# All four LSTM gates as a tanh, three in one activation, with doubled states, and another order of two loads

## The chip, the cores and the metric

The kernel runs on one core of one Trainium2 chip. The metric is the device time of one execution in microseconds (us), given as the median of several runs. Engines: PE (TensorE: matmuls, PEld are its weight loads), DVE (VectorE), ACT (ScalarE), POOL (GpSimd) and SP (SyncE). SP, ACT and POOL also issue DMAs.

## The reference

The input x has 1250 rows of 512, and there is a list of 20,000 edges (src, dst). Each row is normalised, goes through a two-layer graph network (sums over edges, two 512x512 weight products per layer), and is added to x. The result, normalised again, is the input sequence of an LSTM with 1250 steps, batch 1 and 512 hidden values; its outputs are added and returned. The LSTM is what the change touches:

```python
combined = jnp.concatenate((x_t, h_prev), axis=1)
f_t = jax.nn.sigmoid(combined @ W_f + b_f)
i_t = jax.nn.sigmoid(combined @ W_i + b_i)
c_tilde = jnp.tanh(combined @ W_c + b_c)
c_t = f_t * c_prev + i_t * c_tilde
o_t = jax.nn.sigmoid(combined @ W_o + b_o)
h_t = o_t * jnp.tanh(c_t)
```

## The kernel before, in words

**Graph part (0 to about 390 us).** Edge counts are built as matmuls of one-hot rows, then two layers of aggregation (L784) and weight products (L176). During it POOL and SP load the input weights Wx of the four gates and their biases bx (`load_wx`, L570 and L572); POOL's next own instruction after these is the first write to xp_d.

**The LSTM in 32 stretches.** The 1250 rows are cut into 32 stretches of 40 that run side by side, as a batch of 32. Each stretch begins 96 steps ahead of its own rows so that its state settles: 12 steps without the recurrent product (BEFORE) and 84 with it (WARM). So there are 84 + 40 = 124 full steps, n = -84 to 39. At the end the kept states of neighbouring stretches are compared against TOL; `far` holds the count of values further apart, and only if that count is over 0 does the branch of L1094 run all 1250 steps in order (`in_order`). Every engine reads that count (L1092) for the branch.

**Input products.** The product of the normalised rows with Wx is made in 40 units: 10 tiles of 128 rows, each with 4 quarters of the 512 hidden values. `multiply(u)` makes one on PE (8 matmuls at L970, and four transposes per tile at L888). `put(u, part)` adds the bias on DVE (L980) and splits the result into three bf16 planes: L982 on ACT, L986 on DVE, L987 on ACT, L989 on DVE, one waiting for the other; then POOL writes them to xp_d in DRAM (L990). `fetch(n)` on SP (L855) reads the planes of one step n back for all stretches. It must wait until all four quarters of a tile are written. At most five fetched steps are held.

**The stretch before the recurrence.** The order of all engines in the LSTM is written out by hand. The first 19 units (AHEAD) run alone; from unit 7 on, each has one of the 12 steps without recurrence beside it: PE opens it from a fetched step (L1003), ACT applies tanh and sigmoid (L1010, L1012), DVE updates the cell (L1014, L1015), and then the splitting of the unit before follows on the same engines. At the end of each iteration ACT issues one of 16 loads of the recurrent weights Wh (L618, 256 KB each; gate by gate, four parts a gate). The first full step reads all of Wh.

**A full step.** The 512 hidden values lie as four column groups of 32 partitions with 128 values each, cut into two halves s = 0, 1 of 64. `open_gates` (L630) brings in the input products, `add_gates` (L638) adds the recurrent product in eight blocks. The blocks come in the order

```python
for b, s in ((0, 0), (1, 0), (0, 1), (2, 0), (3, 0), (1, 1), (2, 1), (3, 1)):
```

where blocks b = 0, 1 read hT[0], the transposed output of the first half, and b = 2, 3 read hT[1]. So the three blocks up to (0, 1) need hT[0] alone, the next wants hT[1], the gates of the first half are complete after five blocks, and those of the second after eight. Each block is 4 matmuls in two passes, 8 matmul records. Then `cell` runs for each half: ACT tanh of gate c (L645), sigmoid of f and i (L647), sigmoid of o (L649); DVE two products in one instruction (L651), their sum (L652); ACT tanh of the new state (L654); DVE the output (L655) and its transpose to hT (L656). DVE and ACT work strictly in this order, so the second half's L651 stands behind the first half's L656. For the first 21 full steps (units 19 to 39) a `multiply` and a `put` stand beside the step. From n = 0 on DVE also adds the output to the rows (L1089), and rows are stored in six groups (L865), the last after the last step.

**Places.** `gates` (L149) sets the order of the gates in Wx, bx, Wh and in the step's PSUM tile: f, i, o, c. The state cg holds two blocks of 64: cell state and tanh of c.

Of the kernel before, what the change touches and what calls it, by code (L numbers as in the profile page):

```python
# [38 lines left out]
def gnn_lstm_kernel(  # L39
# [44 lines left out]
    def rsqrt(pool, v, out, name):  # L84
# [9 lines left out]
        nc.vector.tensor_scalar(q, q, -0.5, 1.5, OP.mult, OP.add)  # L94
# [54 lines left out]
    gates = [(W_f, b_f), (W_i, b_i), (W_o, b_o), (W_c, b_c)]  # L149
# [6 lines left out]
    def layernorm_scale(pool, mv, out, name):  # L156
        ve = pool.tile([R, mv.shape[1]], F32, name=name + "_v")
        nc.vector.tensor_scalar(ve, mv[:, :, 1], EPS, None, OP.add)
        rsqrt(pool, ve, out, name)
# [47 lines left out]
    with ExitStack() as gnn_stack:  # L207
# [358 lines left out]
        def load_wx(pool):  # L566
            Wx = pool.tile([128, KD, NG, D], F32, name="Wx")
            bx = pool.tile([R, NG, D], F32, name="bx")
            for g, (W, b) in enumerate(gates):
                (nc.sync if g % 2 else nc.gpsimd).dma_start(  # L570
                    Wx[:, :, g, :], W[:D, :].rearrange("(k p) n -> p k n", p=128))
                nc.gpsimd.dma_start(bx[:, g, :], row_bcast(b, R))  # L572
            return Wx, bx
# [21 lines left out]
        def rstd_of(pool, t0, n):  # L595
            layernorm_scale(pool, mv2[:, t0:t0 + n, :], rstd2[:, t0:t0 + n], f"lx{t0}")
# [14 lines left out]
        def load_wh(pool):  # L611
# [11 lines left out]
            return Wh, [lambda g=g, j=j: part(g, j) for g in range(NG) for j in range(4)]  # L623
# [17 lines left out]

        def cell(pool, p, cg, s, hh, hT):

            m = slice(64 * s, 64 * (s + 1))
            nc.scalar.activation(cg[:, 1, :], p[:, 3, :], AF.Tanh)  # L645
            sg = pool.tile([128, 2, 64], F32, name=f"sg{s}")
            nc.scalar.activation(sg, p[:, 0:2, :], AF.Sigmoid)  # L647
            so = pool.tile([128, 64], F32, name=f"so{s}")
            nc.scalar.activation(so, p[:, 2, :], AF.Sigmoid)  # L649
            pr = pool.tile([128, 2, 64], F32, name=f"pr{s}")  # L650
            nc.vector.tensor_mul(pr, sg, cg)  # L651
            nc.vector.tensor_add(cg[:, 0, :], pr[:, 0, :], pr[:, 1, :])  # L652
            th = pool.tile([128, 64], F32, name=f"th{s}")
            nc.scalar.activation(th, cg[:, 0, :], AF.Tanh)  # L654
            nc.vector.tensor_mul(hh[:, m], so, th)  # L655
            nc.vector.transpose(hT.rearrange("p b c -> p (b c)"), hh[:, m])  # L656

        def in_order(pool, ps_g, Wh):

            cgs = [pool.tile([128, 2, 64], F32, name=f"cgs{s}") for s in range(2)]  # L660
# [4 lines left out]
            with tc.For_i(0, N, 1) as t:  # L665
# [20 lines left out]
                nc.vector.tensor_add(xr, xr, hh)  # L686
# [6 lines left out]
        def general():  # L693
# [64 lines left out]
            with tc.tile_pool(name="any_lstm", bufs=1) as anyp, \  # L758
                    tc.tile_pool(name="any_ps", bufs=1, space=PSUM) as ps_g:
                Wh, parts = load_wh(anyp)  # L760
                for part in parts:
                    part()
# [130 lines left out]
        def lstm(first_yT, Wx, bx, Wh, wh_parts, close_wx):  # L893
# [7 lines left out]
            TOL, CHECK = 2.0 ** -18, 3  # L901
# [7 lines left out]
            with ExitStack() as pools:  # L909
# [7 lines left out]
                cgs = [seq.tile([128, 2, 64], F32, name=f"cg{s}") for s in range(2)]  # L917
# [79 lines left out]
                cx = some.tile([128, 2, 128], F32, name="cx")  # L997
# [9 lines left out]
                def step_before(final):  # L1007

                    p = opened.pop(0)
                    nc.scalar.activation(cx[:, 1, :], p[:, 3, :], AF.Tanh)  # L1010
                    sg = some.tile([128, 2, 128], F32, name="sgx")
                    nc.scalar.activation(sg, p[:, 0:2, :], AF.Sigmoid)  # L1012
                    pr = some.tile([128, 2, 128], F32, name="prx")
                    nc.vector.tensor_mul(pr, sg, cx)  # L1014
                    nc.vector.tensor_add(cx[:, 0, :], pr[:, 0, :], pr[:, 1, :])  # L1015
# [3 lines left out]
                    nc.scalar.activation(pr[:, 0, :], p[:, 2, :], AF.Sigmoid)  # L1019
                    nc.scalar.activation(pr[:, 1, :], cx[:, 0, :], AF.Tanh)  # L1020
                    nc.vector.tensor_mul(hh, pr[:, 0, :], pr[:, 1, :])
# [5 lines left out]
                with tc.manual_schedule(engines={mybir.EngineType.PE, mybir.EngineType.DVE,  # L1027
                                                 mybir.EngineType.Activation, mybir.EngineType.Pool,
                                                 mybir.EngineType.SP}):

                    nc.scalar.activation(warm, ones, AF.Sigmoid)
# [13 lines left out]
                    for u in range(AHEAD):  # L1045
# [10 lines left out]
                        for part in wh_parts[u:u + 1]:  # L1056
# [4 lines left out]
                    for n in range(-WARM, LEN):  # L1061
# [25 lines left out]
                        if n >= 0:  # L1087

                            nc.vector.tensor_add(x2c[:, n, :], x2c[:, n, :], hh)  # L1089
                            if n + 1 in stores:  # L1090
                                store(x2c, ([0] + stores)[stores.index(n + 1)], n + 1)
                n_far = nc.values_load(far, min_val=0, max_val=128 * 8 * 31)  # L1092
# [14 lines left out]
        def fast():  # L1107
            with ExitStack() as side, ExitStack() as right:
# [13 lines left out]
                Wh, parts = load_wh(late)  # L1122
                lstm(first_yT[0], Wx, bx, Wh, parts, right.close)
# [35 lines left out]
```

## Time and profile before

| | us |
|---|---|
| median of 3 runs | 1097.77 (1097.53 to 1098.74) |
| the profiled execution, whole | 1097.48 |
| its span, first to last instruction | 1095.7 |
| PE busy | 1008.4 (92%) |
| DVE busy | 520.5 (48%) |
| ACT busy | 342.8 (31%) |
| POOL busy | 57.9 (5%) |
| PE busy from 471.0 to 629.6 | 156.7 of 158.6 |
| PE busy from 629.6 to 1085.5 | 399.3 of 455.9 |
| granted TensorE clock, mean | 0.992 |

How to read the rows that follow. A row of a group gives line, engine, operation, written tile <- read tiles, partitions x elements, count, then busy time in us, mean ns of one, and after the second bar the idle time of that engine just before these instructions, with what ended it. A row in order of time gives start in us, length in us, and in square brackets how long the engine had been idle and who released it; PEld rows show when PE's weight loads begin, which is when the data for the matmuls was there. Matmul ends are modelled, so a busy PE may hold small gaps. A wait row gives the total, the number and the longest. "adj", "planes", "S" and "h" are names of memory that the LSTM uses again for its own tiles.

### The profile page before, as it was taken

Reading aid. Unit: us, or ns where it says so; the run is one execution under the profiler, and the core shown is the slowest. Engines: PE = TensorE matmul, PEld = TensorE weight load, DVE = VectorE, ACT = ScalarE, POOL = GpSimd, SP = SyncE. Lnnn points to the kernel's source line nnn. Section 1 sums busy time; section 2 is a strip of 40 time slices with the busy share of each in tenths; the row PEclk is TensorE's granted clock in tenths of the full one; section 3 lists DMA queues with packets and bytes.
Section 4 is the critical chain, followed back from the end, with each engine's and each line's share of the span. In section 5 each row is a group of like instructions: output and inputs, shape, how many; then the busy total and the mean of one; then the engine's idle time right before and its main releaser. Section 6 shows DMA issues by size and latency. Waiting matters only on the chain.

```text
span 1095.7 us, 26606 instructions
## 1 busy us (share of the span) xinstructions
PE 1008.4 (92%) x10972; PEld 520.2 (47%) x10988; DVE 520.5 (48%) x1800; ACT 342.8 (31%) x1268; POOL 57.9 (5%) x96
## 2 busy tenths in 40 slices
PE   7999999999999998999999988888888888888886
PEld 4555554554455443344444444444444444444443
DVE  7887676003300765655554544444444444444444
ACT  3321224204301024433333333333333333333332
POOL 0000001000000011111101070000000000000000
PEclk9999999999999999999999999999999999999999
DMA  8100001500200047663323383333333333434441
GB/s 251 50 1 1 0 1 69 204 1 25 69 1 1 0 126 245 188 186 101 95 90 109 102 227 103 89 91 90 91 96 89 88 88 89 109 82 123 108 96 21
DMA packets 38227, 98.51 MB, mean 90 GB/s; under 512 B 5796, under 2 KB 11756, under 8 KB 38094
## 3 DMA queue, kind: packets, MB, share of 16 engines
q1 hardware_dynamic: 28208, 68.67, 22.7%
q0 software_dynamic: 7168, 23.60, 6.3%
q10 hardware_dynamic: 2718, 4.42, 1.3%
q8 instruction: 89, 1.46, 0.5%
q14 instruction: 44, 0.36, 0.1%
HBM read 74.29 MB, written 19.76 MB: 86 GB/s over the span
## 4 chain that ended last, share of the span: by engine, by line
PE 50%; issue 26%; DVE 13%; ACT 7%; DMA 1%; SPq 1%; POOL 1%; DVEq 0%; ACTq 0%; POOLq 0%
PE gates L638 29%; PE psM L970 8%; PE psM L176 8%; DVE adj L651 3%; ACT adj L654 3%; DVE hT L656 3%; DVE adj L655 2%; DVE cg L652 2%; ACT cg L645 2%; PE acc L441 2%; ACT adj L647 2%; DVE od L427 1%; POOL xp_d L990 1%; PE gates L630 1%; DVE ob L425 1%
## 5 line engine op out<-in xcount | busy, mean ns | idle before, releaser
L638 PE MATMUL gates<-Wh,hT 128*32 128x256 f32 x7936 | 457.6, 381 | 58.3 <-DVE hT L656 58.1
L638 PEld LDWEIGHTS gates<-Wh,hT 128*32 128x32 f32 x7936 | 233.4, 109 | 254.1 <-DVE hT L656 119.6
L651 DVE TENSOR_TENSOR adj<-adj,cg 128x128 f32<-128x128 f32 x248 | 68.2, 275 | 222.9 <-ACT adj L647 222.5
L970 PE MATMUL psM<-Wx,xT 128*128 128x512 f32 x320 | 147.4, 606 | 0.6 <-DVE adj L980 0.6
L784 PE MATMUL agg<-adj,planes 128*128 128x512 bf16 (+1 forms) x704 | 129.1, 343 | 2.7 <-DVE x L489 1.9
L645 ACT ACTIVATE cg<-gates 128x64 f32<-128x64 f32 x248 | 55.4, 223 | 213.5 <-PE gates L638 209.9
L654 ACT ACTIVATE adj<-cg 128x64 f32<-128x64 f32 x248 | 63.6, 256 | 129.5 <-DVE cg L652 129.5
L784 PEld LDWEIGHTS <-planes 128*128 128x128 bf16 x720 | 70.4, 98 | 62.4 <-DVE x L489 2.7
L655 DVE TENSOR_TENSOR adj<-adj 128x64 f32<-128x64 f32 x248 | 55.9, 225 | 79.9 <-ACT adj L654 79.9
L970 PEld LDWEIGHTS psM<-Wx,xT 128*128 128x128 f32 x320 | 58.7, 192 | 71.3 <-issue 69.0
L656 DVE STREAM_TRANSPOSE hT<-adj 128x64 f32<-128x64 f32 x248 | 60.8, 245 | 23.7 <-DVE adj L655 0.9
L647 ACT ACTIVATE adj<-gates 128x128 f32<-128x128 f32 x248 | 67.2, 271 | 0.1
L652 DVE TENSOR_TENSOR cg<-adj 128x64 f32<-128x64 f32 x248 | 55.8, 225 | 8.5
L176 PE MATMUL psM<-w,hT 128*128 128x512 f32 x128 | 58.6, 610 | 0.0
L649 ACT ACTIVATE adj<-gates 128x64 f32<-128x64 f32 x248 | 57.0, 230 | 0.0
L427 DVE TENSOR_SCALAR od<-ids,key 125x820 f16<-125x820 f16 (+42 forms) x160 | 55.5, 347 | 0.0
L630 PE MATMUL gates<-h,sel 96*32 96x256 bf16 x992 | 50.3, 273 | 0.1
L990 POOL DMA_DIRECT2D xp_d<-planes x40 | 28.7, 718 | 408.2 <-issue 214.3
L441 PE MATMUL acc<-od,ob 125*128 125x400 f16 (+22 forms) x360 | 46.1, 260 | 3.6 <-DVE od L427 3.2
L425 DVE TENSOR_SCALAR ob<-ids,low 125x128 f16<-125x128 f16 x160 | 39.5, 247 | 13.5 <-PE acc L441 13.2
L982 ACT CAST planes<-adj 128x512 bf16<-128x512 f32 x40 | 24.7, 618 | 60.7 <-DVE adj L980 60.7
L630 PEld LDWEIGHTS <-sel 96*32 96x32 bf16 x992 | 26.6, 97 | 35.2 <-issue 16.4
(165 smaller groups left out, 704.6 us busy)
## 6 DMA issues: line engine op xcount, KB each, us to landing
h<-xp_d SPq DMA_DIRECT2D x136, 384.0 KB, 4.1
xp_d<-planes POOLq DMA_DIRECT2D x40, 384.0 KB, 3.3
base<-x POOLq DMA_DIRECT2D x40, 64.0 KB, 4.6
w<-in_L_gnn_w_dram SPq DMA_DIRECT2D x2, 1024.0 KB
w<-in_L_gnn_w_dram POOLq DMA_DIRECT2D x2, 1024.0 KB, 5.9
xp_d<-planes SPq DMA_DIRECT2D x10, 144.0 KB, 2.9
h<-in_x_dram SPq DMA_DIRECT2D x10, 128.0 KB, 2.6
h<-in_x_dram SPq DMA_DIRECT2D x10, 120.0 KB, 2.8
```

Of the source, the lines that this page charges most:

```text
L176: nc.tensor.matmul(p, lT[:, k, :], rhs[:, k, :], start=(k == 0), stop=(k == KD - 1))
L630: nc.tensor.matmul(ps[s][32 * j:32 * (j + 1), :, :], lhs(j), rhs(j, s), start=True, stop=False)
L638: nc.tensor.matmul(ps[s][32 * j:32 * (j + 1), :, :], hT[b // 2][:, b % 2, :], Wh[:, b, :, 128 * j + 64 * s:128 * j + 64 * (s + 1)], start= ...
L645: nc.scalar.activation(cg[:, 1, :], p[:, 3, :], AF.Tanh)
L647: nc.scalar.activation(sg, p[:, 0:2, :], AF.Sigmoid)
L651: nc.vector.tensor_mul(pr, sg, cg)
L652: nc.vector.tensor_add(cg[:, 0, :], pr[:, 0, :], pr[:, 1, :])
L654: nc.scalar.activation(th, cg[:, 0, :], AF.Tanh)
L655: nc.vector.tensor_mul(hh[:, m], so, th)
L656: nc.vector.transpose(hT.rearrange("p b c -> p (b c)"), hh[:, m])
L784: nc.tensor.matmul(p[:, :n * R], planes[:, k, pl, f * 128:(f + 1) * 128], adj[:, k, t0:t0 + n, :].rearrange("b i r -> b (i r)"), start=(k ...
L970: nc.tensor.matmul(p, yT[n][:, k, :], quarter(Wx[:, k, :, :], j), start=(k == 0), stop=(k == KD - 1))
```

## The change

Four things are done.

1. **Gates as a tanh.** sigmoid(z) = (1 + tanh(z/2)) / 2. All gates are now tanh with a constant scale, the cell state is kept as 2c and the output as 2h. To make one scale serve all gates, the pre-activations come out as 2z for f, i, o and 4z for c: rstd2 is doubled, bx is doubled, and for gate c Wx, bx and Wh are doubled once more. The order of gates becomes f, i, c, o, so that f, i, c are next to each other: one activation writes all three into cg, which has four blocks now (state, f, i, c). Gate o has an activation of its own, as before. DVE's products, sum, output and the adding to the rows become scalar_tensor_tensor (two operations with a constant in one instruction); their number is the same. The tolerance of the comparison doubles with the states.
2. **Doublings.** POOL doubles bx and the parts for gate c right after their loads (three instructions). ACT doubles Wh's part for gate c in four instructions, one at the end of each of units 4 to 7. In the built order the fourth stands between unit 7's splitting and the next step without recurrence.
3. **Loads of Wh.** Two parts at the end of each of units 0 to 4 (gate c first), none in units 5 to 10, one in each of units 11 to 16. Before: one in each of units 0 to 15.
4. **The count.** Every engine reads `far` after the last step's adding and before the last stores; before, after them.

In the built program one activation table for tanh is loaded in the stretch before the recurrence, in place of two (tanh, then sigmoid). W_c moves from SP's to POOL's queue and W_o the other way, since the gates alternate.

```diff
-    gates = [(W_f, b_f), (W_i, b_i), (W_o, b_o), (W_c, b_c)]
+    gates = [(W_f, b_f), (W_i, b_i), (W_c, b_c), (W_o, b_o)]
+    C, O = 2, 3
...
+            for v in (bx, bx[:, C, :], Wx[:, :, C, :]):
+                nc.gpsimd.tensor_scalar(v, v, 2.0, None, OP.mult)
...
+            def double(b):
+                nc.scalar.activation(Wh[:, b, C, :], Wh[:, b, C, :], AF.Copy, scale=2.0)
...
+        def inner(p, cg, pr, so=None):
+            nc.scalar.activation(cg[:, 1:4, :], p[:, 0:3, :], AF.Tanh, scale=0.25)
+            if so is not None:
+                nc.scalar.activation(so, p[:, O, :], AF.Tanh, scale=0.25)
+            nc.vector.scalar_tensor_tensor(pr, cg[:, 1:3, :], 1.0, cg[:, 0:4:3, :],
+                                           op0=OP.add, op1=OP.mult)
+            nc.vector.scalar_tensor_tensor(cg[:, 0, :], pr[:, 0, :], 0.5, pr[:, 1, :],
+                                           op0=OP.mult, op1=OP.add)
+        def outer(hh, cg, so, th):
+            nc.scalar.activation(th, cg[:, 0, :], AF.Tanh, scale=0.5)
+            nc.vector.scalar_tensor_tensor(hh, so, 1.0, th, op0=OP.add, op1=OP.mult)
+        def add_rows(x, hh):
+            nc.vector.scalar_tensor_tensor(x, hh, 0.5, x, op0=OP.mult, op1=OP.add)
...
         def cell(pool, p, cg, s, hh, hT):
-            nc.scalar.activation(cg[:, 1, :], p[:, 3, :], AF.Tanh)
-            sg = pool.tile([128, 2, 64], F32, name=f"sg{s}")
-            nc.scalar.activation(sg, p[:, 0:2, :], AF.Sigmoid)
             so = pool.tile([128, 64], F32, name=f"so{s}")
-            nc.scalar.activation(so, p[:, 2, :], AF.Sigmoid)
             pr = pool.tile([128, 2, 64], F32, name=f"pr{s}")
-            nc.vector.tensor_mul(pr, sg, cg)
-            nc.vector.tensor_add(cg[:, 0, :], pr[:, 0, :], pr[:, 1, :])
             th = pool.tile([128, 64], F32, name=f"th{s}")
-            nc.scalar.activation(th, cg[:, 0, :], AF.Tanh)
-            nc.vector.tensor_mul(hh[:, m], so, th)
+            inner(p, cg, pr, so)
+            outer(hh[:, m], cg, so, th)
             nc.vector.transpose(hT.rearrange("p b c -> p (b c)"), hh[:, m])
...
-            TOL, CHECK = 2.0 ** -18, 3
+            TOL, CHECK = 2.0 ** -17, 3
...
                 def step_before(final):
                     p = opened.pop(0)
-                    nc.scalar.activation(cx[:, 1, :], p[:, 3, :], AF.Tanh)
-                    sg = some.tile([128, 2, 128], F32, name="sgx")
-                    nc.scalar.activation(sg, p[:, 0:2, :], AF.Sigmoid)
                     pr = some.tile([128, 2, 128], F32, name="prx")
-                    nc.vector.tensor_mul(pr, sg, cx)
-                    nc.vector.tensor_add(cx[:, 0, :], pr[:, 0, :], pr[:, 1, :])
+                    inner(p, cx, pr)
...
-                        for part in wh_parts[u:u + 1]:
+                        for part in wh_parts[2 * u:2 * u + 2] if u < 5 else wh_parts[u - 1:u]:
+                            if u < 5 or u > 10:
+                                part()
+                        for part in wh_doubles[u - 4:u - 3] if u >= 4 else ():
                             part()
...
                         if n >= 0:
-                            nc.vector.tensor_add(x2c[:, n, :], x2c[:, n, :], hh)
+                            add_rows(x2c[:, n, :], hh)
+                            if n + 1 == LEN:
+                                n_far = nc.values_load(far, min_val=0, max_val=128 * 8 * 31)
                             if n + 1 in stores:
                                 store(x2c, ([0] + stores)[stores.index(n + 1)], n + 1)
-                n_far = nc.values_load(far, min_val=0, max_val=128 * 8 * 31)
```

In the new kernel the wide activation stands at L654, the output gate's at L656, the products at L657, the sum at L659, the tanh of the state at L664, the output at L665 and the transpose at L678.

## The prediction

> **What bounds the kernel now.** I read the page for the lines that carry time, then PE's waits by stretch, then one step in order of time. The last half of the span is the recurrence: 124 steps. 21 of them (471 to 630 us) have 3.6 us of input products beside them; PE then lacks 1.9 us in all, so nothing off PE counts there. The other 103 (n = -63 to 39) do not:
>
> ```profile
> L638 PE MATMUL gates<-Wh,hT 128*32 128x256 f32 x7936 | 457.6, 381 | 58.3 <-DVE hT L656 58.1
> ...
> L645 ACT ACTIVATE cg<-gates 128x64 f32<-128x64 f32 x248 | 55.4, 223 | 213.5 <-PE gates L638 209.9 <-PE gates L630 0.6
> ...
> L647 ACT ACTIVATE adj<-gates 128x128 f32<-128x128 f32 x248 | 67.2, 271 | 0.1
> ```
>
> PE waits 58 us for the transposes L656, ACT 210 us for PE: a loop, each waiting for the other. One step in order of time (start, length):
>
> ```profile
> 807.29 1.88 PEld L638 LDWEIGHTS gates<-Wh,hT 128*32 128x32 f32 x40 [0.31 <-DVE hT L656]
> ...
> 808.49 0.22 ACT L645 ACTIVATE cg<-gates 128x64 f32<-128x64 f32 x1 [1.86 <-PE gates L638]
> 808.61 0.27 ACT L647 ACTIVATE adj<-gates 128x128 f32<-128x128 f32 x1
> ...
> 808.91 0.29 DVE L651 TENSOR_TENSOR adj<-adj,cg 128x128 f32<-128x128 f32 x1 [1.68 <-ACT adj L647]
> ...
> 809.24 0.22 DVE L652 TENSOR_TENSOR cg<-adj 128x64 f32<-128x64 f32 x1
> ...
> 809.79 0.23 DVE L655 TENSOR_TENSOR adj<-adj 128x64 f32<-128x64 f32 x1 [0.32 <-ACT adj L654]
> ...
> 810.12 0.25 DVE L656 STREAM_TRANSPOSE hT<-adj 128x64 f32<-128x64 f32 x1
> ...
> 810.29 0.25 DVE L651 TENSOR_TENSOR adj<-adj,cg 128x128 f32<-128x128 f32 x1
> ```
>
> The reader is to see two loops. **First half:** hT[1] reaches PE at 807.29, ACT starts at 808.49, hT[0] reaches PE at 810.42 (3.12 after 807.29); PE then needs 6 groups of 4 matmuls (0.24 + 5 x 0.216 = 1.32) before it wants hT[1]: 4.44 round. **Second half:** 807.29, ACT at 809.78 (ten groups), L651 at 810.29, hT[1] at 811.74: 4.45 round, the step's period. L651 of the second half starts right behind the transpose of the first (810.12 + 0.17), 0.08 later than its activations would allow. So a gain in the first half moves both.
>
> **The steps: three activations become two.** ACT start to L651 is 0.42: L647 starts 0.12 behind L645, takes 0.27, and 0.03 passes. After, one activation of 192 per row stands there. The trace has no such width. The same PSUM form just behind a wait takes 224 ns at 64 (L645), 278 at 128 (L1010), 384 at 256 (L1012): 0.83 ns an element, so 192 takes 331 ns, an estimate from these rows, and L651 starts 0.36 behind: **0.061 us less**. The output gate's own activation still ends (0.46) long before L665 reads it. Bounds: the 64-to-128 step as L645 and L647 show it (224, 271) gives 318 and 0.074 less; an activation that reads SBUF (L1020, 301 at 128) would take 354 at 192, and 0.038 less. I take 331, on the line of three rows of the same form.
>
> The DVE instructions stay four. Three become scalar_tensor_tensor with constants:
>
> ```profile
> L928 DVE TENSOR_TENSOR S<-S 128x248 f32<-128x248 f32 x1 | 0.4, 418 | 0.0
> L929 DVE SCALAR_TENSOR_TENSOR S<-S 128x248 f32<-128x248 f32 x1 | 0.4, 418 | 0.0
> ...
> L187 DVE SCALAR_TENSOR_TENSOR w<-ident,w 128x128 f32<-128x128 f32 x16 | 3.5, 285 | 10.6 <-ACT w L181 10.6
> ```
>
> Same time at 248 a row, and 285 at 128 against 291 for L651: cost nothing. The strided operand (tanh and state, three blocks apart) is read in rows of 64 as before. Each new instruction waits for the same engines as the one it replaces. The scale constants are part of the activation: L482 (scale a constant, 2048 a row) at 1906 ns fits 0.83 ns an element and 0.2 fixed. add_rows is a DVE instruction like L1089 (250 ns), with over 1 us of idle DVE behind it.
>
> Both loops shorten by 0.061: the first half by its activation, the second because the transpose it stands behind comes earlier (its activations would allow 2.86 after 807.29; the transpose allows 2.93). Next late is the same loop; PE's own work per step is 3.73 of 4.39. 103 x 0.061 = **6.3 us** (3.9 by 0.038, 7.6 by 0.074).
>
> [...]
>
> **The stretch before the recurrence (391 to 471 us).** PE makes products, DVE and ACT split them, POOL writes them to xp_d, SP fetches them.
>
> ```profile
> PE pc L1003 <- DMA h<-xp_d: 4.6, 3, 2.8
> PE psM L970 <- DVE adj L980: 0.6, 1, 0.6
> ```
>
> First what PE waited for (total, times, longest), then rows in order of time:
>
> ```profile
> 412.33 1.28 ACT L1010 ACT_TABLE_LOAD   x1
> ...
> 413.92 1.28 ACT L1012 ACT_TABLE_LOAD   x1
> ...
> 432.00 0.57 PE L1003 MATMUL pc<-h,sel 96*32 96x512 bf16 x4 [2.80 <-DMA h<-xp_d]
> 432.50 5.18 PE L970 MATMUL psM<-Wx,xT 128*128 128x512 f32 x8
> ```
>
> Tanh and sigmoid each load a table at 412; with tanh alone one goes (1.28) and the two activations of a step become one (384 a row, about 0.48 against 0.28 + 0.38 + gaps). L1014 comes at 414.1, not 415.63; the 0.6 wait of PE goes. What is late next: L980, L982, L986, L987 and L989 of the same unit follow, then the fourth doubling of Wh, which stands on ACT ahead of the next activation. A doubling is one 128x512 activation, 0.62 (L248). The other three fall into gaps of 1.4 us in front of L982; this one takes 0.6 of the 1.5 gained. The last write of tile 1 to xp_d then leaves about 1.05 earlier than 424.04, and the fetch behind it, which PE waits for at 432.00, lands about 1.05 earlier. After that the same chain runs on: PE's waits of 2.80 and 1.32 stay nearly as long. **1.1 us.**
>
> The uneven Wh loads I cost at nothing: packets of a fetch come 1.3 to 1.4 us after its issue whether a Wh load went just before (407.9, 427.1, 446.2) or not (463.9). Two loads per unit up to unit 4 can delay the write that the first fetch waits for, by at most the 256 KB added, 0.9 us at the 300 GB/s that this stretch reaches; that is the lower bound (0.2 left). Above: behind the wait of 2.80 the products run at half pace (a unit of 5.18, else 3.6), behind that of 1.32 they don't. The wait shrinks to 2.5; if that is short enough, 1.5 us more. I take the nearer row, 2.80.
>
> [...]
>
> POOL's doubling of Wx and bx (4608 a row; by masks' select at 285 ns for 128, 10 us) starts when the last bx load has landed (209 us). Behind it on POOL is L990 at 394.7, and PE's first use is at 386.6: 165 us of cover. W_c and W_o trade the SP and POOL queues, both landed by 209.
>
> **The end.** SP issues its last store until 1091.95, then reads the count (TENSOR_LOAD 0.60, checks, branch at 1092.98), then walks 20 semaphores to the end. Read early, SP does it while it waits for the last row, and ACT behind its last activation (1089.08, done by 1090.0, and its first store goes at 1090.14 anyway). SP comes 0.96 earlier to its semaphores; but the last store, issued at 1091.77, lands 1.8 later, 1093.58, between the second and third of them, so part is waited for again. Between 0 and 0.96; I take **0.4**.
>
> Sum: 6.3 + 1.1 + 0.4 = 7.8. The profiled execution took 1097.48 (span 1095.7 and 1.78 around it): 1089.7. It lies 0.29 under the median of 1097.77: **1090.0 us**.
>
> **Rivals.**
> - *The clock stays up.* The wait for the second fetch, 2.5 in place of 2.80, no longer halves the pace of the products behind it: 1.5 us more, 1088.5. For it: 1.32 didn't; against: 2.80 is nearer. 0.20. [...]
> - *The uneven loads free the fetches.* With no Wh load from unit 5 to 10 they land in time, and PE's waits (4.6 + 0.6) and the half pace (1.5) go: 6.7 in place of 1.1, 1084.4. For it: the 16 DMA engines are full from 410 to 418 and 430 to 438 us; against: the fetch issued at 463.9, with no Wh load near, took as long. 0.10.
> - *The step does not follow.* Another wait takes the place: the second half's L651 stays where it is, so only the stretch before and the end gain, 1.5: 1096.3. For it: that L651 waits behind a transpose, not behind ACT; against: that transpose moves too. 0.05.
> - *Slower: the three DVE instructions cost more than those they replace.* Each lies on both loops. L265 and L586 (a column as scalar) take 747 to 750 at 512 a row, L986 692: 0.055 more. With that, 3 x 0.055 - 0.061 = 0.104 a step: 10.7 us slower, less 1.5: 1107.0. It decides from 0.025 each. Against: L929 and L187 show nothing. 0.03.
> - *It does not do what it says.* The rounding of the tanh form leaves states apart by more than the tolerance, and all 1250 steps run in order, at no less than 4.4 us: over 6,600 us in all. 0.02.
>
> The forecast itself 0.60. Its bounds are 3.9 + 0.2 + 0 = 4.1 (1093.7) and 7.6 + 2.6 + 1.0 = 11.2 (1086.6), the first rival's within them; all ends at once are unlikely above, and the second rival lies below: 1085.5 to 1093.5. What a measurement can tell from no change is 0.2%, 2.2 us. Faster 0.92, same 0.03 (from the third rival), slower 0.05.
>
> **What would show it.** Right: plain steps 4.39 apart; the wide activation 331 ns and L657 0.36 behind its start; L657, L659, L665 at 291, 225, 225; one table load at 412; the second fetch wait about 2.5; no TENSOR_LOAD on SP behind the last store. Wrong: a step over 4.43, L657 longer than 0.30, more than 5 us of fetch waits, or PE matmuls of the first step waiting for Wh.

## The result, and the profile after

| | before | after |
|---|---|---|
| median, us | 1097.91 (1097.53 to 1098.74, 4 runs) | 1089.07 (1087.37 to 1090.95, 4 runs) |
| the profiled execution, whole | 1097.48 | 1087.95 |
| its span | 1095.7 | 1086.0 |
| granted clock, mean | 0.992 | 0.994 |

The ratio is 0.9921 (95% interval 0.9909 to 0.9934): 8.8 us faster. The forecast was 1090.0, with a range of 1085.5 to 1093.5. Five more runs of the changed kernel on another chip gave a median of 1090.5 (1090.34 to 1091.18), again 0.9922 (0.9908 to 0.9936).

The two spans differ by 9.7 us. Cut at the same events of both traces (first Wh load, transposes of the first half of a step):

| stretch | before | after | gain | forecast |
|---|---|---|---|---|
| start to the first Wh load | 390.83 | 390.33 | 0.50 | 0 |
| to the first full step's transpose | 85.20 | 83.01 | 2.19 | 1.1 |
| first 20 full steps | 149.21 | 149.25 | -0.04 | 0 |
| the other steps, to the last step's transpose | 463.13 | 456.01 | 7.12 | 6.3 |
| from there to the end | 7.33 | 7.36 | -0.03 | 0.4 |

**The steps.** From the page's costliest groups, after (line, engine, operation, tiles, count, then busy us and mean ns of one, then idle time ahead and its releaser):

```profile
L648 PE MATMUL gates<-Wh,hT 128*32 128x256 f32 x7936 | 457.4, 381 | 51.2 <-DVE hT L678 51.0
...
L657 DVE SCALAR_TENSOR_TENSOR adj<-cg 128x128 f32<-128x128 f32 x248 | 68.2, 275 | 215.9 <-ACT cg L654 215.6
L654 ACT ACTIVATE cg<-gates 128x192 f32<-128x192 f32 x248 | 82.0, 330 | 221.4 <-PE gates L648 212.3
...
L665 DVE SCALAR_TENSOR_TENSOR adj<-adj 128x64 f32<-128x64 f32 (+1 forms) x249 | 56.1, 225 | 80.5 <-ACT adj L664 80.5
...
L659 DVE SCALAR_TENSOR_TENSOR cg<-adj 128x64 f32<-128x64 f32 x248 | 55.7, 224 | 8.5
```

The reader is to see that PE's idle time ahead of L648 fell from 58.3 to 51.2 us with the same matmuls; that the wide activation takes 330 ns (331 was estimated); and that the three DVE instructions cost what the old ones did (before: L651 275, L652 225, L655 225). One step of after in order of time:

```profile
802.14 1.88 PEld L648 LDWEIGHTS gates<-Wh,hT 128*32 128x32 f32 x40 [0.30 <-DVE hT L678]
803.34 0.33 ACT L654 ACTIVATE cg<-gates 128x192 f32<-128x192 f32 x1 [1.86 <-PE gates L648]
...
803.70 0.29 DVE L657 SCALAR_TENSOR_TENSOR adj<-cg 128x128 f32<-128x128 f32 x1 [1.61 <-ACT cg L654]
...
806.53 1.88 PEld L648 LDWEIGHTS gates<-Wh,hT 128*32 128x32 f32 x40 [0.31 <-DVE hT L678]
```

L657 starts 0.36 behind the activation (0.42 before), and 806.53 - 802.14 = 4.39 is the period (4.456 before, 4.395 after, medians).

**The stretch before the recurrence.** PE's waits there, after (total, times, longest):

```profile
PE pc L1025 <- DMA h<-xp_d: 3.0, 2, 2.2
```

Before, 4.6 with 2.80 the longest. That looks like the small gain that was forecast; it is another picture. PE in order of time, after:

```profile
413.41 0.40 PE L1025 MATMUL pc<-h,sel 96*32 96x512 bf16 x4 [2.22 <-DMA h<-xp_d]
413.74 5.40 PE L992 MATMUL psM<-Wx,xT 128*128 128x512 f32 x8
419.07 0.40 PE L1025 MATMUL pc<-h,sel 96*32 96x512 bf16 x4
419.40 3.70 PE L992 MATMUL psM<-Wx,xT 128*128 128x512 f32 x8
...
431.60 0.40 PE L1025 MATMUL pc<-h,sel 96*32 96x512 bf16 x4
```

The rows of before at the first fetch, and of after for the table load on ACT:

```profile
412.12 0.40 PE L1003 MATMUL pc<-h,sel 96*32 96x512 bf16 x4 [0.43 <-DMA h<-xp_d]
```

```profile
411.83 1.28 ACT L654 ACT_TABLE_LOAD   x1
```

The wait of 2.2 us stands at the first fetch (413.41), where before had 0.43; the second fetch, 2.80 before, is waited for 0.14 (431.60). The unit at half pace (5.40 in place of 3.70) moved with the long wait, from 432.5 to 413.74. The table load is single, as forecast, and runs from 411.83 to 413.11: all of it lies inside the new wait (411.19 to 413.41).

### The profile page after: what moved, and what is told of

Read it like the earlier page. It is cut to its first block, busy times and chain, and to the rows that moved or that the text cites. A ratio compares the mean times of both kernels' runs of the same rounds, so it can differ in the third digit from the quotient of the medians.

```text
span 1086.0 us, 26341 instructions
## 1 busy us (share of the span) xinstructions
PE 1006.8 (93%) x10972; PEld 520.6 (48%) x10988; DVE 520.8 (48%) x1800; ACT 327.7 (30%) x1011; POOL 70.5 (6%) x99
## 4 chain that ended last, share of the span: by engine, by line
PE 68%; DVE 15%; ACT 7%; issue 5%; DMA 2%; SPq 1%; POOL 0%; ACTq 0%; DVEq 0%; POOLq 0%
PE gates L648 29%; PE psM L180 14%; PE agg L806 12%; PE psM L992 8%; ACT cg L654 3%; DVE adj L657 3%; ACT adj L664 3%; DVE hT L678 3%; DVE adj L665 2%; DVE cg L659 2%; PE acc L445 2%; DMA h<-xp_d 1%; DVE od L431 1%; PE gates L640 1%; DMA base<-in_x_dram 1%
## 5 line engine op out<-in xcount | busy, mean ns | idle before, releaser
L648 PE MATMUL gates<-Wh,hT 128*32 128x256 f32 x7936 | 457.4, 381 | 51.2 <-DVE hT L678 51.0
L648 PEld LDWEIGHTS gates<-Wh,hT 128*32 128x32 f32 x7936 | 233.4, 109 | 246.6 <-DVE hT L678 112.1
L657 DVE SCALAR_TENSOR_TENSOR adj<-cg 128x128 f32<-128x128 f32 x248 | 68.2, 275 | 215.9 <-ACT cg L654 215.6
L654 ACT ACTIVATE cg<-gates 128x192 f32<-128x192 f32 x248 | 82.0, 330 | 221.4 <-PE gates L648 212.3
L664 ACT ACTIVATE adj<-cg 128x64 f32<-128x64 f32 x248 | 63.6, 256 | 129.8 <-DVE cg L659 129.8
L665 DVE SCALAR_TENSOR_TENSOR adj<-adj 128x64 f32<-128x64 f32 (+1 forms) x249 | 56.1, 225 | 80.5 <-ACT adj L664 80.5
L678 DVE STREAM_TRANSPOSE hT<-adj 128x64 f32<-128x64 f32 x248 | 60.8, 245 | 23.3 <-DVE adj L665 0.5
L659 DVE SCALAR_TENSOR_TENSOR cg<-adj 128x64 f32<-128x64 f32 x248 | 55.7, 224 | 8.5
L656 ACT ACTIVATE adj<-gates 128x64 f32<-128x64 f32 x248 | 53.9, 218 | 0.0
L445 PEld LDWEIGHTS <-ob 125*128 125x128 f16 x360 | 29.0, 98 | 25.3 <-issue 11.0
```

Source lines behind the costliest of these rows:

```text
L445: nc.tensor.matmul(blocks[i][:, (d0 - i * BW) * T:(d1 - i * BW) * T], ob, od[:, (d0 - lo) * T:(d1 - lo) * T], start=False, stop=last)
L648: nc.tensor.matmul(ps[s][32 * j:32 * (j + 1), :, :], hT[b // 2][:, b % 2, :], Wh[:, b, :, 128 * j + 64 * s:128 * j + 64 * (s + 1)], start= ...
L654: nc.scalar.activation(cg[:, 1:4, :], p[:, 0:3, :], AF.Tanh, scale=0.25)
L657: nc.vector.scalar_tensor_tensor(pr, cg[:, 1:3, :], 1.0, cg[:, 0:4:3, :], op0=OP.add, op1=OP.mult)
L659: nc.vector.scalar_tensor_tensor(cg[:, 0, :], pr[:, 0, :], 0.5, pr[:, 1, :], op0=OP.mult, op1=OP.add)
L664: nc.scalar.activation(th, cg[:, 0, :], AF.Tanh, scale=0.5)
```

## The experiments

Each row is one profiled execution. "Write 3" is the write to xp_d of unit 3, which the first fetch waits for; "write 7" the same for the second. The opens are the PE matmuls that wait for the first, second and third fetch. The last column is the first full step's transpose, counted from the first Wh load. "After, again" is experiment 11; the other rows are experiments 8, 1, 2, 12, 5, 6, 9 and 10. All in us, from the traces.

| kernel | write 3 to issue of fetch 1 | waits at opens 1, 2, 3 | unit behind open 1 / 2 | write 7 behind open 1 | fetch 2 to open 2 | first full step |
|---|---|---|---|---|---|---|
| before | 3.17 | 0.43, 2.80, 1.32 | 3.96 / 5.61 | 11.92 | 4.87 | 85.20 |
| after | 4.61 | 2.22, 0.14, 0.80 | 5.66 / 3.96 | 11.09 | 4.03 | 83.01 |
| after, again | 4.29 | 2.77, 0.15, 0.62 | 5.66 / 3.96 | 11.09 | 4.03 | 83.40 |
| before, uneven loads | 5.00 | 2.18, 0.61, 1.19 | 5.66 / 3.96 | 11.15 | 4.44 | 83.96 |
| after, even loads | 3.18 | 0.59, 2.93, 0.51 | 3.96 / 3.96 | 10.59 | 5.58 | 82.17 |
| after, four fillers | 4.78 | 0, 0.59, 1.12 | 3.96 / 3.96 | 9.69 | 4.18 | 83.23 |
| after, two fillers | 5.05 | 0.65, 0.79, 1.13 | 3.96 / 3.96 | 9.69 | 4.38 | 82.43 |
| parted loads | 3.19 | 0.97, 1.81, 1.17 | 3.96 / 3.96 | 10.86 | 4.20 | 82.41 |
| parted, table early | 3.19 | 1.49, 0.77, 1.03 | 3.96 / 3.96 | 9.57 | 4.46 | 81.75 |
| loads on SP | 3.07 | 0.36, 1.88, 0.64 | 3.96 / 3.96 | 10.82 | 4.33 | 81.04 |
| loads on SP, table early | 3.07 | 0.56, 0.48, 0.26 | 3.96 / 3.96 | 9.39 | 4.38 | 79.48 |

Experiments 3, 4 and 7 leave this stretch as it is in the changed kernel, and their first full step came at 83.19, 83.46 and 85.16. With the two rows of after, the same code took 83.0 to 85.2 us in five executions; in the longest the first fetch took 6.04 us to reach PE, in the others 4.54 to 5.39. A difference of less than some 2 us between two single rows is therefore not firm by itself.

**1. Even loads.**

```diff
-   for part in wh_parts[2 * u:2 * u + 2] if u < 5 else wh_parts[u - 1:u]:
-       if u < 5 or u > 10:
-           part()
+   for part in wh_parts[u:u + 1]:
+       part()
```

> Only the loads of Wh differ from the changed kernel: one per unit in units 0 to 15, as before the change, gate c still first. Theory: the pairs of loads in units 0 to 4 hold up the write of unit 3 to xp_d (4.34 us from issue to landing in the changed kernel, 2.90 before), so the first fetch is issued 1.0 us late, PE waits 2.22 us for it and runs the next unit at half pace (5.0 us in place of 3.4). With one load per unit that write lands within 3.0 us, PE waits less than 1 us for the first fetch and unit 7 takes 3.4 to 3.6 us; the wait for the second fetch, 0.14 in the changed kernel, is 1.3 to 2.0 us. In all 0 to 2 us faster than the changed kernel, the more if no unit runs at half pace. Rival: the late write is scatter from run to run; then write, wait and half pace stay, and the time is that of the changed kernel within 0.5 us.

Measured: 1088.67 us (1087.57 to 1090.04), ratio to before 0.9914 (0.9901 to 0.9928). The write, the first wait and the pace came as the theory had them. The second wait is longer than expected, 2.93: with a Wh load issued 0.73 us ahead of it, the fetch takes 5.58 us to reach PE, against 4.03. This is the wait that the prediction forecast for the changed kernel (2.5): it belongs to even loads. And it did not halve the pace; the last section says what the traces show on this. PE around it:

```profile
430.83 0.40 PE L1025 MATMUL pc<-h,sel 96*32 96x512 bf16 x4 [2.93 <-DMA h<-xp_d]
431.16 3.70 PE L992 MATMUL psM<-Wx,xT 128*128 128x512 f32 x8
```

**2. The wait filled with matmuls.** In `open_before`, ahead of the first step only (4 here, 2 in experiment 12):

```diff
+   for k in range(4 if not opens else 0):
+       nc.tensor.matmul(p, yT[1][:, k, :], quarter(Wx[:, k, :, :], 3), start=True, stop=True)
+   opens.append(1)
```

> The changed kernel with four more matmuls of 128x512 (0.43 us each, their results are overwritten) on PE ahead of the first step without recurrence, where PE waits 2.22 us. Theory: the half pace behind the wait comes from PE standing still. Then unit 7 takes 3.4 to 3.6 us in place of 5.0, everything behind follows by 1.6 us (the write that the second fetch waits for follows PE), and the kernel is 1.6 us faster than the changed one. Rival 1: the half pace comes with the transfers or with the new stage, not with PE standing still; the unit still takes 5.0 and the time stays. Rival 2: unit 7 runs at full pace, but the wait for the second fetch grows from 0.14 to 1.7 and takes it back: time unchanged.

Measured: 1088.98 us (1088.38 to 1089.54), 0.9911 (0.9895 to 0.9926). The half pace is gone (3.96 in place of 5.66), so it does come from PE standing still. The expected 1.6 us did not come (first full step at 83.23). I had taken a record for a matmul: one is two records, so the four took 3.6 us in place of 1.7, past the fetch, and the first open came 1.1 later. What was left went into the second and third waits (0.59 and 1.12), much as the second rival had it.

> The changed kernel with two added matmuls (four records, 1.7 us) ahead of the first step without recurrence, in place of the four (3.6 us) that ran past the fetch. Theory: PE stands still for 0.3 to 1.1 us only, unit 7 runs at full pace, so the next step without recurrence is opened 3.96 us behind the first in place of 5.66. The write that the second fetch waits for has ACT's chain ahead of it too (about 10.0 us behind the first open, 11.1 in the changed kernel), so of the 1.7 some 1.1 us is left at the second fetch: first full step 81.7 to 82.3 behind the first Wh load, 0.7 to 1.3 us faster than the changed kernel. Rival: everything behind the first open is set by the fetches alone; then the second wait takes the whole back, and the first full step stays at 83.0 to 83.4.

Measured: 1088.28 us (1086.82 to 1089.0), 0.9906 (0.9892 to 0.992). First full step at 82.43, just past the range of the theory and outside the rival's: 0.6 to 1.0 earlier than in the two executions of the changed kernel. Of the 1.7 us of half pace 0.6 to 1.0 would come through by this; the rest is taken back by the later fetches (waits 0.79 and 1.13). The interval of the time overlaps that of the changed kernel, and one trace lies only 0.6 under the shortest of the five executions of the unaltered stretch, so a gain is likely but not shown. PE there:

```profile
411.44 1.88 PE L1025 MATMUL pc<-Wx,xT 128*128 128x512 f32 x4
413.98 0.40 PE L1029 MATMUL pc<-h,sel 96*32 96x512 bf16 x4 [0.65 <-DMA h<-xp_d]
414.31 3.70 PE L992 MATMUL psM<-Wx,xT 128*128 128x512 f32 x8
```

**3. The count read late.** `values_load` moved back behind the last stores.

> The changed kernel with the count read behind the last stores, as before the change. Theory: SP's walk over its semaphores begins when the last store has landed, 1.7 us after its issue in both kernels, and the read was already hidden behind that: no change, within 0.2 us. Rival (the prediction): the early read brings 0.4 us, at most 0.96, so this kernel is 0.4 to 1.0 us slower than the changed one, and in its trace the semaphores begin later behind the last store.

Measured: 1089.78 us (1089.42 to 1090.94), 0.9922 (0.9908 to 0.9935): the ratio of the changed kernel. From the last step's transpose to the end 7.39 us, changed kernel 7.36, before 7.33. SP's first semaphore of the end comes 1.75 us behind the issue of ACT's last store here, 1.69 in before, 1.71 in after. Here and in before it follows 0.48 behind SP's branch, in after 1.55 behind: there SP has nothing left to do and still waits. That semaphore is the one of SP's own last store, and it is passed 2.06 (before), 2.09 (after) and 2.12 us (here) behind that store's issue, so by these rows SP waits for the store. The late read is as long as that wait, and hiding it gains nothing.

**4. Three activations.** In a full step; the output gate's activation stays behind them.

```diff
-   nc.scalar.activation(cg[:, 1:4, :], p[:, 0:3, :], AF.Tanh, scale=0.25)
+   nc.scalar.activation(cg[:, 3, :], p[:, C, :], AF.Tanh, scale=0.25)
+   nc.scalar.activation(cg[:, 1:3, :], p[:, 0:2, :], AF.Tanh, scale=0.25)
```

> The changed kernel, but in a full step gate c and gates f, i are two activations of 64 and 128 again, all tanh; everything else as changed. Theory: the whole gain of the steps is the width of the activation: L651's counterpart starts 0.42 behind the first activation again, plain steps go from 4.395 back to 4.456, and the kernel is 6.3 us slower than the changed one (3.9 to 7.6). Rival: part of the gain comes from elsewhere (the order of the gates in PSUM, the scalar_tensor_tensor); then the steps stay below 4.43 and the kernel is less than 3.5 us slower.

Measured: 1096.4 us (1093.28 to 1098.56), 0.9979 (0.9967 to 0.9991). Median period 4.454, and the steps behind the first 20 take 462.87 us in place of 456.01, 6.9 more. So the merging of the two activations carries the gain, all but 0.3 us of it, and the rest of the new form does not. ACT's rows:

```profile
801.47 0.22 ACT L657 ACTIVATE cg<-gates 128x64 f32<-128x64 f32 x1 [1.86 <-PE gates L648]
801.59 0.27 ACT L658 ACTIVATE cg<-gates 128x128 f32<-128x128 f32 x1
```

The products on DVE start at 801.89, 0.42 behind the first, as before the change.

**7. One activation for four gates**, `activation(cg[:, 1:5, :], p, AF.Tanh, scale=0.25)`.

> The changed kernel, but in a full step all four gates go through one activation of 256 per row, in place of 192 and 64. Theory: the loop pays for the width of the activation that the products wait for, 0.83 ns an element and row: 64 more are 0.053 us, plain steps 4.448 apart in place of 4.395, 5.5 us slower. Rival 1: one instruction fewer on ACT pays for it; steps stay 4.395 apart and the time is that of the changed kernel. Rival 2: the sum of the step's two activations counts, not the first: they overlap by 0.1, so the step is 0.07 shorter.

Measured: 1095.17 us (1093.87 to 1097.21), 0.9961 (0.9947 to 0.9976). Median period 4.451, the same steps 461.96, 6.0 us more. Both rivals fall. The group on the page:

```profile
L657 ACT ACTIVATE cg<-gates 128x256 f32<-128x256 f32 x248 | 94.8, 382 | 214.7 <-PE gates L648 210.7
```

382 against 330: the loop pays for the 64 values that nobody waits for yet.

**8. The uneven order in the kernel before.** The diff of experiment 1 the other way, in before.

> The kernel before the change with nothing but the uneven order of the Wh loads (two per unit up to unit 4, none from 5 to 10, one from 11 to 16; gates in the old order). Theory: the order alone costs at the first fetch (write of unit 3 lands 1.0 to 1.6 us later, PE waits 2 to 3 us in place of 0.43) and gains at the second (3.9 to 4.2 us from issue to landing in place of 4.7), with a table load hidden behind the first wait; in sum 0.5 us slower to 1 us faster. Rival (the prediction's second): the fetches of units 5 to 10 are free, the waits go from 4.6 to under 2 us and the kernel is over 2.5 us faster.

Measured: 1096.92 us (1095.61 to 1098.9), 0.9979 (0.997 to 0.9989). By the ratio 2.3 us faster (1.2 to 3.3), more than the theory's 1; in the profiled executions the first full step comes 1.2 us earlier. What makes up the difference between the two is not shown. Write 3 lands late, PE waits 2.18 in place of 0.43, and the half pace moves from the second wait to the first. The new wait hides one of the two table loads (412.78 to 414.06, the open at 414.33), and the second fetch reaches PE in 4.44 in place of 4.87. The rival's picture falls, since PE still waits 4.0 us in all. The theory's terms stand, but its gain was too small.

**5 and 6. Loads parted around the fetches.** Load counts by unit `{0: 3, 1: 3, 2: 1, 6: 1, 7: 2, 10: 1, 11: 2, 14: 1, 15: 2}`; 6 adds an activation of one value at the end of unit 2, which loads the table there, and takes each doubling one unit earlier.

> The changed kernel with the 16 loads of Wh issued 3, 3 and 1 at the end of units 0, 1, 2, then 1 and 2 at units 6 and 7, 10 and 11, 14 and 15: none in the units just ahead of a write that a fetch waits for, or of that fetch. Theory: a Wh load in flight delays the write or the fetch behind it (second fetch 5.4 us from issue to landing with a load ahead of it in the kernel with even loads, 3.9 without in the changed one; write of unit 3 4.3 against 2.9). Then the first wait is under 0.8, the second about 1.4, the third under 0.8, and the first full step begins 80.2 to 81.0 us behind the first Wh load (83.0 in the changed kernel, 82.2 with even loads): 2 to 2.8 us faster than the changed kernel. Rival: the landing times are set by the traffic of the fetches and writes themselves; then the waits add up to 4 us as with even loads, and the stretch takes 82 us or more.

> As the kernel with parted loads, and besides the table of tanh is loaded at the end of unit 2 by an activation of one value, in idle time of ACT, and each doubling of Wh comes one unit earlier (the last no longer stands ahead of the write that the second fetch waits for). Theory: with the first wait short, the table load of 1.28 us stands between the first fetch and that write, and the doubling takes 0.6; without them the write leaves 1.2 to 1.9 us earlier, the second wait falls under 0.5, and the first full step begins 79.2 to 79.8 behind the first Wh load: 3.2 to 3.8 us faster than the changed kernel. Rival: the write follows PE, not ACT; then nothing beyond the parted loads is gained.

Measured: 1089.22 us (1087.1 to 1090.26), 0.9901 (0.9884 to 0.9919), and 1087.9 (1086.62 to 1088.24), 0.9892 (0.9876 to 0.9908). Both theories miss: 82.41 and 81.75 in place of 80.2 to 81.0 and 79.2 to 79.8. The transfers did what was expected (3.19 and 4.20), but ACT pays for issuing loads in a row. The numbers of experiment 5's rival came out (waits of 3.95 in all, a stretch over 82), but not its reason: fetch 2 reached PE in 4.20, where even loads took 5.58. The rival of experiment 6 falls: write 7 leaves 9.57 behind the open in place of 10.86. ACT in the kernel with parted loads (ACTq is its DMA issuing):

```profile
418.51 1.11 ACTq L624 DMA_DIRECT2D Wh<-in_L_ffn_W_i_dram  x2
419.67 0.63 ACT L630 ACTIVATE Wh<-Wh 128x512 f32<-128x512 f32 x1 [0.55 <-issue]
```

ACT stands idle for 0.55 us until the two issues are through; only then does the next activation start. In unit 0, three in a row put the first write at 4.36 behind the first load, 3.88 with two (the changed kernel) and 3.62 with one (experiment 1). The writes up to unit 3 keep that delay: it leaves at 14.42, in the changed kernel at 13.93.

**9 and 10. Loads on SP.** `nc.scalar.dma_start` of Wh becomes `nc.sync.dma_start`, with counts `{0: 8, 4: 3, 8: 3, 12: 2}`, behind the fetches of these units; 10 adds the table load at the end of unit 1 and the earlier doublings. 11 is the changed kernel, on the same chip.

> The changed kernel with the loads of Wh issued by SP instead of ACT: 8 ahead of everything at unit 0, 3 behind the first fetches (unit 4), 3 at unit 8, 2 at unit 12. Theory: in the kernels with parted loads ACT itself paid for issuing two or three loads in a row (the second takes 0.44 to 0.76 us, and the casts behind it wait), so the writes left late. From SP, behind the fetches, the loads cost neither: write of unit 3 leaves 13.9 us behind the first load or earlier, first wait under 0.6, second under 1.5 (the table load and a doubling still stand ahead of its write), third under 0.8; first full step 80.5 to 81.5 behind the first load, 1.5 to 2.5 us faster than the changed kernel. Rival: eight loads at once fill the DMA engines and the first writes to xp_d land late; then the first wait is 2 us or more again and nothing is gained.

> As the kernel with the loads on SP, and the table of tanh loaded at the end of unit 1 and each doubling one unit earlier. Theory: the write that the second fetch waits for leaves about 1.2 us earlier and all three waits stay under 0.8; first full step 79.2 to 80.2 behind the first load; 3 to 3.8 us faster than the changed kernel, so about 1085.5 where the changed one has 1089. Rival: the write follows PE and not ACT; no more than the loads on SP alone.

> The changed kernel unaltered, on the same chip as the two others. Theory: the spread of its times (1087.4 to 1091.0) comes from PE running at half pace behind a wait in some executions and not in others, and goes with the granted clock of the execution: the time falls by about 1.1 us for 0.001 of mean clock. Rival: it comes from the DMAs; then time and clock are unrelated. Median 1088 to 1090.5.

Measured: 1087.72 (1087.15 to 1088.12), 0.9894 (0.9877 to 0.9911); 1085.75 (1085.53 to 1086.82), 0.988 (0.9863 to 0.9897); 1090.5 (1090.34 to 1091.18), 0.9922. The second stands 4.7 us under the changed kernel on the same chip, their times do not overlap, and it beats both kernels. The first full steps (81.04 and 79.48) lie in the ranges expected; the second wait of experiment 9, 1.88, is longer than the 1.5 expected. The table load of experiment 10, and all of PE's waits for fetches up to 472 us:

```profile
393.51 1.28 ACT L1079 ACT_TABLE_LOAD   x1
```

```profile
PE pc L1025 <- DMA h<-xp_d: 1.3, 3, 0.6
```

Eight loads at once did make the first writes late (8.5 us from issue to landing for unit 0), but that of unit 3 lands in 2.92 and is the one that counts. Experiment 9 against 10 shows what the table load and the fourth doubling cost together, since both were moved: write 7 leaves 10.82 behind the open with the two in the path, 9.39 without, and the second wait falls from 1.88 to 0.48. How much of it is the table alone was not tried.

**Scatter.** In experiment 11 all five runs had the same clock, so it says nothing on its own; its median of 1090.5 is the upper end of what was expected. All nine runs of the changed kernel: two at clock 0.994 took 1087.4 and 1088.0, seven at 0.992 took 1090.2 to 1091.2. Of the 41 runs of before beside experiments 1 to 11, 39 took: 1101.1 on average at 0.990 (5), 1099.5 at 0.991 (14), 1098.6 at 0.992 (16), 1097.3 at 0.993 (4). The other two took 1098.3 at 0.994 and 1095.3 at 0.995. From 0.990 to 0.993 that is 1.25 us for 0.001 on average (0.8 to 1.6 by step), and 1.5 in the changed kernel. The traces show the clock halving for 3.41 us at a time (in after also for two in a row, 28.13 to 34.96); one such time lowers the mean by 0.0016 and cost 1.7 us where it was measured, so 1.1 us for 0.001 (an estimate from these rows). One place is the products near 166 us, identical in all kernels. Windows there, before and after (PE, PEld, DVE, ACT, POOL busy with counts, granted clock, DMA share, GB/s):

```profile
160.00:175.00 15.00, 15.00 (x51) 7.88 (x50) 9.53 (x23) 4.82 (x11) 0.00 (x0) 0.89 0.01 1
```

```profile
160.00:175.00 15.00, 15.00 (x63) 8.39 (x61) 10.85 (x25) 6.26 (x13) 0.00 (x0) 1.00 0.01 1
```

The profiled execution of after had full clock there, and is one of the two short ones.

## Why the prediction came out right, by its own steps

- **The steps: three activations become two (6.3).** Right, mechanism and size: 0.061 of median period, 103 times. Experiments 4 and 7 change only how the gates are cut into activations, to either side, and the period follows. The stretch gained 7.1; the other 0.8 lies in a few irregular steps (together 2.57 us over the median period before, 1.79 after, leaving out the first of the 103). They come and go with the three activations (2.51 in experiment 4); why was not tried.
- The row of the old pair held: in experiment 4 the second activation starts 0.12 behind the first, and the products that read its result start at 0.42.
- **The DVE instructions at nothing.** Right: 275, 224, 225 ns against 275, 225, 225. The rival in which they cost more falls. Its row L986 at 692 was a rare value: the 40 instructions take 648 to 693 ns, median 651.
- **The stretch before the recurrence (1.1, measured 2.2 in the profiled pair).** Two steps failed here and partly made up for each other. "The uneven Wh loads I cost at nothing", with only a loss of 0.9 as a bound: they gain (1.2 us in the traces of experiment 8, 2.3 by its times). The lower bound's mechanism was real and larger than I bounded it: pairs of loads ahead put the first fetch 4.1 to 5.1 us behind write 3 in all eight executions that have them, 3.1 to 3.2 in the six that don't, so 0.9 to 2.0 later. But I did not follow it on: the wait that it opens hides a table load, and ACT and DVE catch up. And the second fetch, with no load just ahead, reaches PE in 4.0 to 4.5 us in twelve executions (4.87 and 5.58 in the two with one). A load ahead is not all that slows a fetch: the first fetch took 4.1 to 6.0 us in the eleven executions that issue none in the 5 us ahead of it and in which PE waits for it. I had read "1.3 to 1.4 us until the first packets" as the whole effect; PE waits for the last packet: in the kernel before the second fetch lands 4.7 us behind its issue, and PE starts at 4.87.
- The rest, 2.19 - 1.24 = 0.95, is what the single table and the single activation of the changed kernel add to the uneven order. It is near the forecast's 1.1, but not the same step: "the wait shrinks to 2.5" was 0.14. Experiment 1 splits the 2.19 the other way round: with even loads the changed kernel comes 3.03 before the kernel before, 1.65 of it because no unit runs at half pace there. That leaves 1.4 for the table and the activation, with write 7 leaving 1.33 earlier behind the open (forecast 1.05), and 0.8 for the uneven loads. Both splits rest on single executions, which scatter by up to 2 us here. As far as they tell, the step forecast at 1.1 is borne out in size, and the one put at nothing is not.
- **The clock rival.** Behind 2.22 the pace halved, so 2.5 would not have escaped by its length. Yet behind 2.93 it did not (experiment 1). The table in the last section shows that it depends on where a wait falls: by it a wait of 2.5 us keeps the pace when the edge of a clock window falls into its middle 1.1 us, which is about one execution in three (an estimate, with 1.8 us as the line and each place of the edge equally likely). So the rival could come true in one run and not in the next.
- **The uneven loads free the fetches.** Half true: it names the second fetch's gain, but not the first fetch's loss. 6.7 was far off.
- **The end (0.4, measured 0).** I saw the last store land between two of SP's semaphores and thought SP's walk was only partly held by it. The rows of after show that the first of them already waits, and experiment 3 that the read fits into this wait. That the whole still came within 1 us of the forecast is in part luck: 0.4 too much here, against too little in the two stretches above.
- **The start** (0.5 in the profiled pair, nothing forecast) goes with the clock at 166 us, not with the change: the three executions that kept full clock there (after, experiments 1 and 4) reach the first Wh load at 390.1 to 390.3, the eleven others at 390.8 to 392.4. In the medians it is mixed with all such places.
- POOL's doublings took 5.37, 5.35 and 1.49 us (12.2, forecast 10), done by 220 us, with the first write at 394.2: hidden, as said. The step did not stay, and the branch was not taken.

## What to carry to other kernels

In a loop between two engines, pay on the path only for what the next instruction reads: one activation of 192 beat two of 64 and 128 (4.395 us a step against 4.454), and one of 256 lost most of what was gained (4.451). Bulk loads that have time belong behind the transfers that an engine waits for, on a queue whose engine has nothing else to do (on SP 1087.72 us, in place of 1090.5 on the same chip); look at the write that the transfer waits for, too (write 3 to the issue of fetch 1: 4.61 us in after, 3.17 before), and at the last packet, not the first (4.7 us and 1.4 behind the issue in the second fetch of before). Put table loads and other side work where their engine is idle anyway, and not between one fetch and the write that the next fetch waits for (the second wait 0.48 in place of 1.88, experiments 10 and 9). Compare more than one trace of a stretch that waits for DMAs before reading a difference of 1 us from it (the same code took 83.0 to 85.2 us).

## What the runs showed of the hardware

- **Half pace behind a wait goes with how much of the wait falls into one clock window.** The traces hold every change of the granted clock. In each of the 14, all changes after the first lie a whole number of times 3.413 us apart (to 0.002 us), and where this grid lies differs from execution to execution. Behind a wait the clock halves for one such window of 3.41 us, which costs 1.7 us (5.66 in place of 3.96). The ten waits over 1.8 us in the stretch before the recurrence:

| wait of PE, us | execution | idle in one window, at most | next window |
|---|---|---|---|
| 3.27 | experiment 7 | 2.79 | half |
| 2.93 | experiment 1 | 1.72 | full |
| 2.80 | before | 2.80 | half |
| 2.77 | experiment 11 | 2.77 | half |
| 2.22 | after | 2.22 | half |
| 2.18 | experiment 8 | 1.98 | half |
| 2.03 | experiment 4 | 2.03 | half |
| 1.89 | experiment 3 | 1.86 | half |
| 1.88 | experiment 9 | 1.48 | full |
| 1.81 | experiment 5 | 1.61 | full |

The wait of 2.77 lies in one window, and the next has clock 0.50; that of 2.93 is cut by an edge at 429.12, and the clock stays at 1.00. Windows of experiment 11, then of experiment 1 (length, busy time of PE, PEld, DVE, ACT and POOL with counts, granted clock, DMA share, GB/s):

```profile
412.34:415.75 3.41, 0.64 (x6) 0.43 (x6) 0.00 (x0) 2.05 (x3) 0.64 (x1) 1.00 0.84 252
415.75:419.17 3.42, 3.42 (x5) 1.35 (x4) 2.01 (x4) 1.24 (x3) 0.00 (x0) 0.50 0.87 265
```

```profile
425.70:429.12 3.42, 2.21 (x9) 0.96 (x7) 2.08 (x5) 1.20 (x3) 0.72 (x1) 1.00 0.85 198
429.12:432.53 3.41, 1.70 (x7) 0.81 (x8) 1.32 (x3) 1.01 (x3) 0.72 (x1) 1.00 1.00 319
```

In this stretch the line lies between 1.72 and 1.86 us of idle time in one window. It is read from ten waits; no run moved a wait against the grid on purpose. It does not hold everywhere as it stands: in experiment 1 a window at 183 us with 1.95 us of idle PE kept the clock, and the halving at 166 us follows a window in which the profile shows no idle PE. With work on PE during the wait the clock was not halved behind it (experiments 2 and 12: waits of 0 and 0.65, units of 3.96 in place of 5.66).
- **ACT's DMA issues cost more in a row** (loads of Wh): one alone 0.32 us, a second one right behind it 0.44 to 1.67, and the activations behind them wait (ACT idle for 0.55 us in experiment 5).
- **A table load of tanh that stands early in the code** ran at 190.9 us, and the square root's table came back at 351.9; it had no effect on the load at 411.83. Put behind the last square root (experiments 6 and 10) it removed that load.
